# Seven and nine single rows in every step, from step -2 on, in a graph network's message passing

## The chip, the cores and the metric

The kernel runs on one core of a Trainium2 chip. The metric is the time of one execution on the device, in microseconds (us). Several executions are timed and the median is given; one more is recorded by the hardware profiler, and the profile is of that one. Engines are named as in the profile: PE is TensorE (matrix products), DVE is VectorE, ACT is ScalarE, POOL is GpSimd, SP is SyncE. SP, ACT and POOL also issue transfers (DMAs); a transfer's issue occupies the issuing engine's own instruction stream, the data move on their own.

## The reference

A graph has 12500 nodes with 64 features (`x`) and 200000 edges, sorted by target node (`dst`). Every edge computes a message from the features of its two ends and from its own 64 features, and the messages are summed at the target:

```python
nodes = node_state[edges].reshape(num_edges, -1)          # x[src], x[dst]: 128 values
gates = ssp(edge_state @ We1 + be1) @ We2 + be2
gates = gates * (1.0 - sigmoid(5.0 * (edges_distance - 3.5)))
h = ssp(nodes @ Wn1 + bn1) @ Wn2 + bn2
messages = h * gates
message_sum = zeros.at[edges[:, 1]].add(messages)
new_state = node_state + (ssp(message_sum @ Ws1 + bs1) @ Ws2 + bs2)
out = layernorm(x + new_state)
```

Here `ssp` is softplus less ln 2. What matters for the change is `x[src]`: the sources are random, so 200000 rows of 64 floats (256 bytes) have to be fetched one by one from memory. The targets are sorted, so neighbouring edges share a narrow window of nodes.

## The kernel before, in words

**Tiles and steps.** The edges are cut into 391 groups of 512 (`GE`); a group is one step `g`. A group has four tiles of 128 edges (`K = 4`), one edge to a partition. The last group has 192 edges of padding, and one of its tiles is padding alone.

**How the source rows come.** `gather(g)` lets POOL issue an indirect DMA for each of the four tiles (line 230): 128 row numbers from `src_i`, 128 rows of `x` into the tile `xg`. In the loop it is called 14 steps ahead (`AHEAD`); the gathers of steps 0 to 13 are issued in the preparation. For steps 5 to 17 the gather's tile is first touched by a small clearing on DVE (line 223, `after=True`), so that the gather takes its place behind what DVE did before. There are 18 buffers, and a later gather waits until the scatter of the step 18 back has read its buffer.

**Tiles by single rows.** Some tiles are not gathered by POOL. For these *slots* the rows are fetched one at a time by plain DMAs of 256 bytes from the queues of SP and ACT into a tile `xr` of their own (`fetch`, lines 232 to 255). Each row's byte address lies in a register; the registers are filled by an instruction that reads some values of `rows_i` from on-chip memory (the helper called at line 244 of the profile, `TENSOR_LOAD` there), and each DMA issue follows a short register move. Before the change a *piece* is four rows (`ROWS = 4`) with one reading of four values. SP fetches (3i + 4)//2 pieces up to step i, so one or two a step and six rows on the mean; ACT two pieces, eight rows, in each step. Both begin at step 0. `slots_by_rows` gives the slots: queue 0 (SP) takes tile 3 of a step, queue 1 (ACT) tile 2, always of the first step that lies at least 8 (SP) or 12 (ACT) steps (`READY`) behind the step in which the 128th row is issued. That makes 17 slots of SP and 23 of ACT, 40 in all, and 1523 gathers are left to POOL.

Each queue has two `xr` tiles, used in turn; the first row of a slot waits until the transposes of the slot two before have read the tile (`behind(ins, ("rows read", n - 2))`). The rows count up one of four semaphores for each queue (`landed`), and the transposes wait for the full count. `onehot` copies the tile's one-hot columns into `xr` on DVE (line 288).

**What a step computes.** `transposes(g)` (PE, line 299; line 296 for a slot's tile) turns rows and one-hot targets; `xcopy` (ACT, line 304) brings them to `xT`. `layer1_bias`, `layer1_edge` and `layer1_node` (PE, lines 309, 314, 320) make the first layer of both networks in `z`; the part of the target node comes from a window of 42 rows of a table made in the preparation, loaded for each half step as `wns` (SP, line 278; a register from `base_i`, line 273, says where). `exps` (ACT, 331), `logs` (ACT, 334) and `softplus` (DVE, 339) make the softplus; `layer2_edge` and `layer2_node` (PE, 345 to 354) the second layer; `hcut` and `message` (DVE, 363, 367) the message; `scatter` (PE, 371) and `window` (DVE, 388) add it to `sums`. When all edges of a block of 512 nodes are through, the parts of `node_block` are spread over the following steps.

**Order.** The order on each engine is the program's order, written out by hand (`tc.manual_schedule()`); an engine takes its instructions one after the other and stands still at one that has to wait. Loop step i, from -3 on, holds the first layer of step i+1, the transposes of step i+3, the second layer of step i and the scatter of step i-3. The first matmul of loop step i takes the waits for `xcopy(i+1)`, `load(i+1)` and gather and one-hot of step i+3. `load(i+5)` (SP) comes at the head of the loop step, `fetch` on SP follows it. On ACT the rows lie between the activations: two before `logs`, two after it, four after `xcopy`. The last ten steps (`CATCH_UP`) have another order and hold no fetches.

Of the kernel before, what the change touches and what calls it, by code (L numbers as in the profile page):

```python
# [44 lines left out]
I32 = mybir.dt.int32  # L45
U8 = mybir.dt.uint8
# [11 lines left out]
P = 128  # L58
D = 64
# [6 lines left out]
K = 4  # L66
# [7 lines left out]


BLOCK_STEPS = ((2, 3, 4, 4, 6, 7, 8, 9, 10, 14), (2, 3, 3, 4, 5, 6, 7, 8, 9, 10), (1, 2, 1, 2, 3))
ROWS = 4
READY = (8, 12)
LANDED = 4
CUTOFF = 5.0  # L80
# [20 lines left out]
    return steps  # L101


def pieces_by_row(i, queue):

    return max(0, 2 * i + 2 if queue else (3 * i + 4) // 2)
# [12 lines left out]


@with_exitstack
def gnn_resnorm_kernel(ctx: ExitStack, tc: tile.TileContext, a: dict, out: bass.AP, E: int):
    nc = tc.nc
    x = a["x"]
    N = x.shape[0]
# [73 lines left out]

    slots = slots_by_rows(NG)  # L200
    by_rows = {(g, k): n for n, (_, g, k) in enumerate(slots)}
    rows_i = const.tile([len(slots), P], I32, name="rows_i")
    queues = (nc.sync, nc.scalar)
    firsts = (0, len([1 for queue, _, _ in slots if queue == 0]), len(slots))
    landed = [[tc.alloc_semaphore(f"rows{queue}_{i}") for i in range(LANDED)] for queue in range(2)]
# [25 lines left out]
                out=xg[:, k, :D], out_offset=None, in_=x,  # L231
                in_offset=bass.IndirectOffsetOnAxis(ap=src_i[:, g, k : k + 1], axis=0)))

    def fetch(i, queue, piece, first=0, count=ROWS):

        if i < 0 or piece >= pieces_by_row(i, queue) - pieces_by_row(i - 1, queue):
            return
        n, r = divmod((pieces_by_row(i - 1, queue) + piece) * ROWS, P)
        n += firsts[queue]
        if n >= firsts[queue + 1]:  # L240
            return
        _, g, k = slots[n]
        if first == 0:
            _, row_at[queue] = nc.values_load_multi_w_load_instructions(  # L244
                rows_i[n : n + 1, r : r + ROWS], engines=[queues[queue].engine], min_val=0, max_val=4 * D * (N - 1),
                skip_runtime_bounds_check_because="src holds rows of x")
        if (n, "in") not in row_tiles:
            row_tiles[n, "in"], xrs[g, k] = row_tile(queue, n), row_tile(queue, n)
        for j in range(first, first + count):
            ins = queues[queue].dma_start(row_tiles[n, "in"][r + j : r + j + 1, :D].bitcast(U8),  # L250
                                          x_bytes[:, bass.ds(row_at[queue][j], 4 * D)])
            tc.no_tile_sem_insts.add(ins.ins.name)
            ins.then_inc(arrived(g, k)[0], 16)
            if r + j == 0:
                behind(ins, ("rows read", n - 2))

    row_at, row_tiles = {}, {}
# [220 lines left out]
    with tc.manual_schedule():  # L478
# [130 lines left out]
        with tc.tile_pool(name="finish", bufs=1) as finish:  # L609
# [24 lines left out]
            for i in range(-3, last - 1):  # L634
                now = parts.pop(i, [])
                early = [part for part in now if part.tensor]
                at(load, i + LOADS)
                fetch(i, 0, 0)
                fetch(i, 0, 1)
                if i >= 0:  # L640
                    at(gather, i + AHEAD, i < BEHIND)
                if i < ends:
                    needs = [("xcopy", i + 1), ("load", i + 1)]
                    needs += [(name, g) for g in ahead[i] for name in ("gather", "onehot")]
                    if i >= -1:
# [24 lines left out]
                    for g in third[i]:  # L670
                        window(g)
                    for part in early:
                        part.others()
                    at(softplus, i + 1)
                else:
                    for g in ahead[i]:
                        transposes(g)
                        xcopy(g)
                    layer1_bias(i + 1)
                    layer1_edge(i + 1)  # L680
                    for part in early:
# [149 lines left out]
def layouts(inputs):  # L831
# [18 lines left out]

    out = {"x": np.ascontiguousarray(x)}
    out["src_l"] = lanes(src, 0)
    out["rows"] = np.ascontiguousarray(out["src_l"].reshape(P, NG, K)[(slice(None), *list(zip(*slots_by_rows(NG)))[1:])].T)
# [45 lines left out]
```

## Time and profile before

| | us |
|---|---|
| median of 3 executions | 1969.16 |
| lowest, highest | 1963.82, 1975.15 |
| profiled execution | 1968.45 |
| its span in the profile | 1966.5 |
| POOL busy, 1523 gathers | 1444.8 |
| PE busy | 1750.5 |
| DVE, ACT busy | 1077.2, 922.5 |

The span is the time from the first to the last instruction that the profiler saw; the execution has 1.95 us around it. The busy time of an engine counts its computing instructions and POOL's gathers; issuing a DMA, register moves and readings of registers are not counted, so SP has no busy time at all, and ACT is occupied for longer than its row says. The page also lists 2176 row DMAs from SP and 2944 from ACT. In the views below, `PEld` is the loading of weights into PE, a `q` behind an engine's name means its instruction stream (ACTq: issued by ACT), and what stands in square brackets is the engine's idle time before the instruction and what ended it.

### The profile page before, as it was taken

How to read it: one execution, taken by the hardware profiler on the slowest of the kernel's cores; microseconds unless marked ns; L12 is line 12 of the kernel's file. 1: busy time of each engine (PE TensorE's matmuls, PEld its weight loads, DVE VectorE, ACT ScalarE, POOL GpSimd, SP SyncE). 2: the span in 40 equal slices, each digit the busy share in tenths (PEclk: the TensorE clock that was granted, in tenths of full speed). 3: DMA queues.
4: the chain of work that ended last, by engine and by line, in shares of the span. 5: the costliest groups of instructions: out<-in, count | busy, mean ns of one | idle time of the engine just before them, and what ended most of it. 6: DMA issues, size and time to landing. Idle time of an engine off the chain costs nothing.

```text
span 1966.5 us, 46634 instructions
## 1 busy us (share of the span) xinstructions
PE 1750.5 (89%) x11373; PEld 1491.4 (76%) x11373; DVE 1077.2 (55%) x2774; ACT 922.5 (47%) x1318; POOL 1445.0 (73%) x1527
## 2 busy tenths in 40 slices
PE   5899999999998988889889988998989989998896
PEld 4777877877777777777777777777777777777775
DVE  4455555555555555555555555555555555555654
ACT  1344545555454444445444444444544454444443
POOL 6777777777777777777777777777777777777770
PEclk9999999999999999999999999999999999999997
DMA  8422222222222222222222222222222222222220
GB/s 242 128 70 65 70 64 72 65 72 65 73 67 73 65 73 67 67 66 69 65 69 66 67 70 67 69 67 70 68 70 73 64 74 68 70 72 71 69 61 13
DMA packets 149240, 143.45 MB, mean 73 GB/s; under 512 B 50073, under 2 KB 96621, under 8 KB 148964
## 3 DMA queue, kind: packets, MB, share of 16 engines
q1 hardware_dynamic: 92972, 88.12, 15.6%
q0 software_dynamic: 48736, 50.00, 11.3%
q10 hardware_dynamic: 7256, 2.27, 0.6%
q8 instruction: 97, 1.59, 0.3%
q14 instruction: 179, 1.47, 0.3%
HBM read 130.59 MB, written 9.63 MB: 71 GB/s over the span
## 4 chain that ended last, share of the span: by engine, by line
PE 46%; ACTq 14%; DMA 10%; SPq 10%; issue 9%; ACT 5%; DVE 3%; POOL 3%; DVEq 0%; POOLq 0%
ACTq L250 11%; PE z L320 10%; PE gh L348 7%; PE gh L354 6%; PE z L314 5%; PE z L371 5%; DMA xg<-in_x,src_i 4%; PE tx L299 4%; DMA wns<-table 4%; SPq L250 4%; ACT u L331 3%; ACTq L244 3%; PE z L309 3%; POOL xg L230 3%; PE gh L345 2%
## 5 line engine op out<-in xcount | busy, mean ns | idle before, releaser
L230 POOL DMA_INDIRECT xg<-in_x,src_i x1523 | 1444.8, 949 | 475.3 <-issue 319.4
L331 ACT ACTIVATE u<-z 128x768 f32<-128x768 f32 x392 | 315.9, 806 | 624.4 <-PE z L371 316.7
L334 ACT ACTIVATE u<-u,one 128x768 f32<-128x768 f32 x392 | 366.0, 934 | 238.5 <-ACT u L331 236.7
L339 DVE SCALAR_TENSOR_TENSOR s<-u,z 128x768 f32<-128x768 f32 x392 | 372.6, 950 | 171.2 <-ACT u L334 154.6
L363 DVE TENSOR_TENSOR h<-gh,cut 128x256 f32<-128x256 f32 x391 | 165.2, 423 | 478.3 <-PE gh L354 472.0
L320 PE MATMUL z<-xT,wns 106*128 106x256 f32 x1564 | 423.9, 395 | 0.0
L354 PE MATMUL gh<-consts,s 128*128 128x64 f32 x3128 | 395.7, 270 | 0.0
L354 PEld LDWEIGHTS gh<-consts,s 128*128 128x128 f32 x3128 | 384.7, 194 | 0.0
L320 PEld LDWEIGHTS z<-xT,wns 106*128 106x128 f32 x1564 | 307.4, 198 | 45.8 <-ACT xT L304 0.7
L348 PEld LDWEIGHTS gh<-consts,s 128*128 128x128 f32 x1564 | 206.7, 192 | 122.8 <-issue 122.3
L348 PE MATMUL gh<-consts,s 128*128 128x128 f32 x1564 | 282.4, 304 | 0.0
L371 PEld LDWEIGHTS z<-xg,msg 128*128 128x128 f32 x1512 | 237.9, 199 | 22.9
L309 PE MATMUL z<-ones,be 3*128 3x256 bf16 x391 | 105.3, 269 | 167.8 <-DMA wns<-table 64.9
L299 PE MATMUL tx<-consts,xg 128*106 128x128 f32 x1524 | 240.8, 280 | 4.0 <-DVE xg L285 2.7
L388 DVE TENSOR_TENSOR sums<-sums,z 64x42 f32 x756 | 148.7, 197 | 171.4 <-ACT u L331 75.2
L314 PE MATMUL z<-eT,consts 128*128 128x256 f32 x782 | 242.4, 393 | 0.0
L304 ACT COPY xT<-tx 106x512 f32<-106x512 f32 x391 | 221.6, 567 | 15.5 <-PE tx L299 15.3
L371 PE MATMUL z<-xg,msg 128*128 128x84 f32 x1512 | 223.3, 271 | 0.0
L309 PEld LDWEIGHTS <-be 3*128 3x128 bf16 x391 | 35.4, 91 | 206.6 <-issue 102.9
L299 PEld LDWEIGHTS tx<-consts,xg 128*106 128x106 f32 x1524 | 181.8, 144 | 5.1 <-DVE xg L285 3.0
L367 DVE TENSOR_TENSOR msg<-gh,h 128x256 f32<-128x256 f32 x391 | 165.9, 424 | 13.4
L345 PE MATMUL gh<-row,ones 3*128 3x512 bf16 x391 | 145.9, 373 | 0.0
(103 smaller groups left out, 714.0 us busy)
## 6 DMA issues: line engine op xcount, KB each, us to landing
eT<-in_eT SPq DMA_DIRECT2D x195, 256.0 KB
xr<-in_x ACTq DMA_DIRECT2D x2944, 0.2 KB
xr<-in_x SPq DMA_DIRECT2D x2176, 0.2 KB
xg<-in_x,src_i POOLq DMA_INDIRECT x1523
wns<-table SPq DMA_DIRECT2D x782, 21.0 KB
table<-tb SPq DMA_DIRECT2D x14, 448.0 KB
sums<-in_xT SPq DMA_DIRECT2D x7, 455.0 KB
y<-in_x SPq DMA_DIRECT2D x24, 128.0 KB
```

Of the source, the lines that this page charges most:

```text
L230: note(("gather", g), nc.gpsimd.indirect_dma_start(out=xg[:, k, :D], out_offset=None, in_=x, in_offset=bass.IndirectOffsetOnAxis(ap=src_i[ ...
L250: ins = queues[queue].dma_start(row_tiles[n, "in"][r + j : r + j + 1, :D].bitcast(U8), x_bytes[:, bass.ds(row_at[queue][j], 4 * D)])
L299: nc.tensor.transpose(tx[:, k, :], xgs[g][:, k, :DW], ident)
L304: note(("xcopy", g), nc.scalar.copy(xT, xTs[g]))
L314: nc.tensor.matmul(zs[g][:, 0, :HE], we1.rearrange("a h d -> a (h d)"), eTs[g], start=False, stop=True, skip_group_check=True)
L320: nc.tensor.matmul(zn, wns[:, g % REST, h, :], xTs[g][:, h], start=True, stop=True, skip_group_check=True)
L331: nc.scalar.activation(us[g][:, part], z_of(g)[:, part], AF.Exp)
L334: nc.scalar.activation(us[g][:, part], us[g][:, part], AF.Ln, bias=one)
L339: nc.vector.scalar_tensor_tensor(ss[g].rearrange("p i t e -> p (i t e)")[:, part], us[g][:, part], BIG, z_of(g)[:, part], OP.min, OP.max)
L348: nc.tensor.matmul(v[:, 0, t], ss[g][:, 0, t, :], we2, start=False, stop=False, skip_group_check=True)
L354: nc.tensor.matmul(ghs[g][:, 1, 2 * t + h, :], ss[g][:, 1 + h, t, :], wn2, start=False, stop=h == 1 and t == 1, skip_group_check=True)
L371: ins = nc.tensor.matmul(sc, msgs[g][:, 2 * t : 2 * t + 2, :].rearrange("p h f -> p (h f)"), xgs[g][:, 2 * t : 2 * t + 2, D:DW], start=t = ...
```

## The change

A piece becomes 7 rows on SP and 9 on ACT (`ROWS`), one piece in every step from step -2 on (`ROWS_FROM`). One reading fills all the registers of a piece; it is a function of its own (`read_rows`), so that on ACT it stands between `exps` and `logs`, two rows behind `logs`, and seven behind `xcopy`. A piece may now run over the end of a slot into the next one. With `READY` as before there are 20 slots of SP and 26 of ACT, 46 in all, and 1517 gathers are left. There are 366 readings on SP and 370 on ACT, for 544 and 736 before. The row numbers lie in `rows_i` by pieces, one partition to a piece: 128 partitions of 48 columns, for 40 partitions of 128.

```diff
-ROWS = 4
+ROWS = (7, 9)
+ROWS_FROM = -2
 READY = (8, 12)
...
-            if pieces_by_row(g - READY[queue], queue) * ROWS >= (n + 1) * P:
+            if (g - READY[queue] - ROWS_FROM + 1) * ROWS[queue] >= (n + 1) * P:
...
+def row_pieces(NG):
+    queues = [queue for queue, _, _ in slots_by_rows(NG)]
+    return [-(-queues.count(queue) * P // ROWS[queue]) for queue in range(2)]
+
+def row_columns(NG):
+    return [-(-n // P) * rows for n, rows in zip(row_pieces(NG), ROWS)]
...
-    rows_i = const.tile([len(slots), P], I32, name="rows_i")
+    pieces_of, columns_of = row_pieces(NG), row_columns(NG)
+    rows_i = const.tile([P, sum(columns_of)], I32, name="rows_i")
...
-    def fetch(i, queue, piece, first=0, count=ROWS):
-        if i < 0 or piece >= pieces_by_row(i, queue) - pieces_by_row(i - 1, queue):
+    def read_rows(i, queue):
+        piece = i - ROWS_FROM
+        if not 0 <= piece < pieces_of[queue]:
             return
-        n, r = divmod((pieces_by_row(i - 1, queue) + piece) * ROWS, P)
-        ...
+        q, p = divmod(piece, P)
+        at = queue * columns_of[0] + q * ROWS[queue]
+        _, row_at[queue] = nc.values_load_multi_w_load_instructions(
+            rows_i[p : p + 1, at : at + ROWS[queue]], engines=[queues[queue].engine], min_val=0,
+            max_val=4 * D * (N - 1), skip_runtime_bounds_check_because="src holds rows of x")
+
+    def fetch(i, queue, first=0, end=None):
+        piece = i - ROWS_FROM
+        if not 0 <= piece < pieces_of[queue]:
+            return
-        for j in range(first, first + count):
+        for j in range(first, ROWS[queue] if end is None else end):
+            n, r = divmod(piece * ROWS[queue] + j, P)
+            n += firsts[queue]
+            if n >= firsts[queue + 1]:
+                return
...
                 at(load, i + LOADS)
-                fetch(i, 0, 0)
-                fetch(i, 0, 1)
+                read_rows(i, 0)
+                fetch(i, 0)
...
                     at(exps, i + 1)
-                    fetch(i, 1, 0, 0, ROWS // 2)
+                    read_rows(i, 1)
                     at(logs, i + 1)
-                    fetch(i, 1, 0, ROWS // 2, ROWS // 2)
+                    fetch(i, 1, 0, 2)
                     for g in ahead[i]:
                         transposes(g)
                         xcopy(g)
-                    fetch(i, 1, 1)
+                    fetch(i, 1, 2)
```

More of the change, by code (lines that the diff above doesn't have):

```diff
@@ L101, in block_steps @@
     return steps
-def pieces_by_row(i, queue):
-    return max(0, 2 * i + 2 if queue else (3 * i + 4) // 2)
 def slots_by_rows(NG):
@@ L232, in gather @@
                 in_offset=bass.IndirectOffsetOnAxis(ap=src_i[:, g, k : k + 1], axis=0)))
-    def fetch(i, queue, piece, first=0, count=ROWS):
-        if i < 0 or piece >= pieces_by_row(i, queue) - pieces_by_row(i - 1, queue):
+    def read_rows(i, queue):
+        piece = i - ROWS_FROM
+        if not 0 <= piece < pieces_of[queue]:
             return
-        n, r = divmod((pieces_by_row(i - 1, queue) + piece) * ROWS, P)
-        n += firsts[queue]
-        if n >= firsts[queue + 1]:
-            return
[L242 to L248, printed above, removed]
-        for j in range(first, first + count):
-            ins = queues[queue].dma_start(row_tiles[n, "in"][r + j : r + j + 1, :D].bitcast(U8),
+        q, p = divmod(piece, P)
[6 more added lines that the diff above has]
+        if not 0 <= piece < pieces_of[queue]:
+            return
+        for j in range(first, ROWS[queue] if end is None else end):
[3 more added lines that the diff above has]
+                return
+            _, g, k = slots[n]
+            if r == 0:
+                row_tiles[n, "in"], xrs[g, k] = row_tile(queue, n), row_tile(queue, n)
+            ins = queues[queue].dma_start(row_tiles[n, "in"][r : r + 1, :D].bitcast(U8),
                                           x_bytes[:, bass.ds(row_at[queue][j], 4 * D)])
@@ L253, in fetch @@
             ins.then_inc(arrived(g, k)[0], 16)
-            if r + j == 0:
+            if r == 0:
                 behind(ins, ("rows read", n - 2))
@@ L852, in layouts @@
     out["src_l"] = lanes(src, 0)
-    out["rows"] = np.ascontiguousarray(out["src_l"].reshape(P, NG, K)[(slice(None), *list(zip(*slots_by_rows(NG)))[1:])].T)
+    rows = []
+    for queue, (n, columns) in enumerate(zip(row_pieces(NG), row_columns(NG))):
+        chosen = [out["src_l"].reshape(P, NG, K)[:, g, k] for q, g, k in slots_by_rows(NG) if q == queue]
+        v = padded(np.concatenate(chosen), P * columns, 0).reshape(-1, P, ROWS[queue])
+        rows.append(v.transpose(1, 0, 2).reshape(P, columns))
+    out["rows"] = np.ascontiguousarray(np.concatenate(rows, axis=1))
     out["dst_l"] = lanes(dst, dst[-1])
```

## The prediction

> **What bounds the kernel now.** I read the busy shares and the costliest groups of the page first, then the gathers and the steps by stretch of time, then the order of single instructions where the stretches change.
>
> ```profile
> PE 1750.5 (89%) x11373; PEld 1491.4 (76%) x11373; DVE 1077.2 (55%) x2774; ACT 922.5 (47%) x1318; POOL 1445.0 (73%) x1527
> ...
> L230 POOL DMA_INDIRECT xg<-in_x,src_i x1523 | 1444.8, 949 | 475.3 <-issue 319.4
> ```
>
> By busy share TensorE (89%) looks like the bound and GpSimd (73%) does not. But GpSimd's idle time of 475.3 us over 1523 gathers is 0.31 us before each one, and most of it waits for nothing the profile knows ("issue"). So a gather costs 0.949 + 0.30 = 1.249 us, start to start. The same groups by stretch, columns: stretch, its length, busy time (instructions), granted clock, DMA share, GB/s; first the gathers, then the copies of `xT`, one for each step:
>
> ```profile
> core 0: us, POOL busy (x), PEclk, DMA share, GB/s
> 90.00:490.00 400.00, 302.56 (x320) 1.00 0.26 68
> 600.00:1000.00 400.00, 302.44 (x320) 0.97 0.26 68
> 1000.00:1400.00 400.00, 302.46 (x320) 0.96 0.27 68
> ```
>
> ```profile
> 90.00:490.00 400.00, 50.95 (x90) 1.00 0.26 68
> 600.00:1000.00 400.00, 46.99 (x83) 0.97 0.26 68
> 1000.00:1400.00 400.00, 46.34 (x82) 0.96 0.27 68
> ```
>
> GpSimd issues 320 gathers in each 400 us, early and late: 1.25 us each, never held up. The steps do change: 90 in 400 us early (4.44 us a step), then 82 or 83 (4.85). A step has 4 gathers less what the rows take over, 6/128 + 8/128 of one: 3.891 x 1.249 = 4.86 us. So until about 520 us the steps eat the lead of the gathers issued in the preparation (step 10 is copied 52 us after its last gather, step 100 nine); from there to about 1885 us GpSimd sets the pace. TensorE's first matmul of a step starts a median 1.9 to 2.3 us after the last gather it needs has left GpSimd, which is the landing (the last gathers are issued 1.3 us before their data arrive). The last gather leaves at 1920.6. The steps after about 1860 are paced by TensorE, ScalarE and VectorE in turn, hang on the gather of step 377, and give 46 us behind the last gather. GpSimd's one large halt is in the beginning:
>
> ```profile
> 79.19 0.94 POOL L230 DMA_INDIRECT xg<-in_x,src_i  x1 [0.30 <-issue]
> 84.75 0.94 POOL L230 DMA_INDIRECT xg<-in_x,src_i  x1 [4.61 <-DVE xg L223]
> ...
> 89.73 0.94 POOL L230 DMA_INDIRECT xg<-in_x,src_i  x1 [0.30 <-issue]
> ```
>
> The gather of step 14 (84.75) waits for VectorE's clearing of its tile, queued behind the first softplus, that behind ScalarE's first exponential. Whatever moves this moment moves the end by as much.
>
> **The change, part by part.** *Six gathers fewer* (46 slots for 40, all before step 380). On a queue that never pauses they are worth 6 x 1.249 = 7.5 us at the last gather. All six lie before the gather at which the last steps stop following GpSimd, so they start 7.5 us earlier too, with the same work: no row is fetched there before or after. Step pace: 3.875 x 1.249 = 4.84 us.
>
> *ScalarE.* Before, with two readings and eight rows:
>
> ```profile
> 1014.27 0.81 ACT L331 ACTIVATE u<-z 128x768 f32<-128x768 f32 x1 [1.52 <-PE z L371]
> 1015.09 0.77 ACTq L250 DMA_DIRECT2D xr<-in_x  x2
> 1015.90 0.94 ACT L334 ACTIVATE u<-u,one 128x768 f32<-128x768 f32 x1 [0.82 <-ACT u L331]
> 1015.98 0.54 ACTq L250 DMA_DIRECT2D xr<-in_x  x2
> 1016.75 0.56 ACT L304 COPY xT<-tx 106x512 f32<-106x512 f32 x1
> 1017.29 1.40 ACTq L250 DMA_DIRECT2D xr<-in_x  x4
> 1018.78 0.81 ACT L331 ACTIVATE u<-z 128x768 f32<-128x768 f32 x1 [1.48 <-DVE s L339]
> ```
>
> 1.63 us from exponential to logarithm, 0.85 to the copy, 2.03 to the next exponential: 4.51. After: only the reading stands before the logarithm, and if it is shorter than the exponential (0.81) the logarithm follows after 0.84, as at the first step, where nothing stood between; two rows lie beside the logarithm (0.84 to the copy); seven rows of 0.313 (1.40 for four, of which 0.23 is the first one's extra behind a reading) take 2.2, with 0.1 around them. Sum 3.98 us: shorter than before, hidden under 4.84. Were that cover gone, the extra row would cost 0.31 a step, less the saved reading. Behind the seven rows queues the next exponential, for which VectorE's softplus and TensorE's second layer wait; that is latency inside a step with 0.8 us to spare.
>
> *SyncE.* A piece of four is reading 0.61 with its gap, 0.07, rows 1.24, 0.05: 1.97 us, 1.5 pieces a step: 2.96. Besides it each step issues half an `eT` load and half a reading of `base_i` (0.45 + 0.54 for two steps), two window loads (0.92), and now and then a `y` or `out` (0.05): 4.41 in all. After: one reading (0.65, next part, and 0.05), 0.07, seven rows (1.24 x 7/4 = 2.17), 0.05: 2.99, in all 4.44. Against 4.84 there is 0.40 to spare. SyncE's window loads are issued a median 29 us before TensorE needs them in the middle, about 10 us early on: either covers the two extra pieces (6 us), and an early delay only shortens the lead that the steps have to use up.
>
> *One reading of seven or nine values* is not in the trace. Columns: least, median, most ns:
>
> ```profile
> L244 ACTq TENSOR_LOAD <-rows_i x736: 478/558/762, 84.0 to 1831.0; - x184
> L244 SPq TENSOR_LOAD <-rows_i x544: 463/564/776, 83.6 to 1791.8; - x182
> ```
>
> ```profile
> L754 ACTq TENSOR_LOAD <-far_i x1: 467/467/467, 1959.9 to 1959.9; - x1
> ```
>
> Four values take 558 or 564 ns, one takes 467 (477 on SyncE): some 30 ns a value more. I take that slope: nine 0.71 us, seven 0.65. Low end: no growth (`base_i`, also four values, has 0.49). High end, time in proportion to values: 1.26 and 0.99. At the high end ScalarE has 3.98 + 1.26 - 0.81 = 4.43 and SyncE 4.78: both still under 4.84, SyncE barely.
>
> The Trainium skill, page "Runtime: NRT & Kernel Launch", section "Instruction fetch mechanics", speaks against this change: register loading costs about 200 ns a register, in its example from HBM. By that rule, as an estimate, a seven-value reading is 1.4 us, SyncE's step 5.19 us, and SyncE would set the pace from 80 us on: 366 pieces end near 1980, and with the 141 us that followed the same step before, the time would be some 2120 us. For four values the rule gives 0.80 us where the row has 0.56, and the numbers here go by the row.
>
> *Two steps earlier.* Each queue gets two more pieces ahead of step 0, where ScalarE stood idle: its copies at 75.27 and 76.12, then nothing until 81.44 (4.74 us, waiting for TensorE). The first nine rows (0.71 + 9 x 0.313 + 0.23 = 3.8 us) fit before 81.44. The second nine push the next exponential from 84.00 to about 85.4 and its logarithm by 0.75, so VectorE's clearing for step 15 goes from 87.67 to about 88.4; GpSimd wants it at 89.73. Bounds: zero, and 7.5 us if both pieces stood whole in GpSimd's way; a gain is excluded, as nothing that the clearing waits for gets shorter. I take zero, by these rows. On SyncE the extra pieces stand behind the loads of steps 0 to 3; the loads of steps 4 and 5 go 3 and 6 us later, to about 87 and 89, for steps near 95 and 99.
>
> *Rows in time, and the rest.* SyncE's pieces of a tile are issued 8 steps before its step, ScalarE's 12; the transposes come 3 before. A tile's first row waits for the tile two slots earlier, whose transposes lie at least five steps back. Six more copies of 0.19 us on VectorE (55% busy), six transposes that read another tile: nothing. Scaling the row numbers over 128x48 for 40x128: nothing.
>
> **Sum.** Span 1966.5 - 7.5 = 1959.0. The profiled execution lasted 1968.45, 1.95 more than its span and 0.7 under the median 1969.16, so its successor is 1961.0, and on the median 1961.7 us (-0.38%).
>
> **Rivals.** *SyncE becomes the bound* (slower). Point: a seven-value reading over 1.05 us (0.65 + 0.40), or as much lost in rows; each 0.1 us beyond costs 366 x 0.1 = 37 us. At 1.2 us: 55 more, about 2017. For it: SyncE's 4.41 of 4.86 is the next fullest queue. Against it: the 30 ns slope. Chance 0.10.
>
> *The beginning eats the gain.* If the earlier pieces stand in GpSimd's way, up to 7.5 us return: 1965 to 1969. For it: a chain of three engines behind 84.75 and only 1.3 us of margin at step 15. Against it: the 4.74 us idle. Chance 0.09.
>
> *The last steps are also quicker.* Behind 1885 TensorE had a mean clock of 0.85 for 81 us, 12 us of full clock withheld; at the middle's 0.97 it would be 2.4. A third of the difference is 3.3 us: 1953 to 1959. Against it: nothing in the change asks for it, and it can as well go the other way. Chance 0.28, the spread of the median included.
>
> **How the numbers follow.** The forecast has 0.53. The range: lowest run less 7.5 and 3.3 is 1953; highest run less 7.5 plus 3.3 is 1971. It leaves out SyncE's case and some edges. A difference within 0.5% (9.8 us) is about what cannot be told from none: faster by more takes the quicker end, 0.28; within, forecast and beginning, 0.62; slower, SyncE, 0.10.
>
> **What would show it.** 1517 gathers at 1.25 us with the last one leaving near 1913 and no new pause; the wait near 79 us as long as before; readings of 0.65 to 0.71 us; the logarithm 0.84 us behind the exponential; 46 us behind the last gather. The prediction is wrong if gathers pause in the middle, if SyncE's window loads come due late, or if step 14's gather starts later than 85.

## The result and the profile after

The changed kernel takes **2286.77 us** (median of 4 executions, 2285.56 to 2295.49), beside 1972.16 us for the kernel before, measured with it (4 executions, 1963.82 to 1979.13): a ratio of 1.161, with a 95% interval of 1.1585 to 1.1644. (The ratios here are the recorded ones; they can differ by up to 0.002 from the quotient of the two medians.) The forecast was 1961.7 us, its range 1953 to 1971. The profiled execution of the changed kernel has a span of 2285.0 us, 318.5 more than before.

The page of the changed kernel, its busy times, the gathers' group and the chain that ended last:

```profile
PE 1935.6 (85%) x11373; PEld 1628.4 (71%) x11373; DVE 1069.1 (47%) x2780; ACT 947.2 (41%) x1318; POOL 1439.9 (63%) x1521
...
ACTq 46%; PE 24%; issue 14%; ACT 12%; DVE 2%; DMA 1%; SPq 0%; DVEq 0%
ACTq L266 29%; ACTq L249 17%; ACT u L347 8%; PE z L336 5%; PE gh L370 4%; PE gh L364 3%; PE z L330 2%; PE z L387 2%; ACT xT L320 2%; PE tx L315 2%; PE z L597 1%; PE gh L361 1%; PE z L325 1%; PE tx L423 1%; ACT u L350 1%
...
L238 POOL DMA_INDIRECT xg<-in_x,src_i x1517 | 1439.7, 949 | 752.4 <-issue 378.6
```

No engine's computing explains 318 us: TensorE's same 11373 matmuls took 185 us more at a lower granted clock, ScalarE's work 25 more. GpSimd issues its 1517 gathers at 949 ns as before but stands idle for 752 us in place of 475. The chain now runs through ScalarE's instruction stream (ACTq), 46% of the span: the row issues of line 266 and, at 17%, the reading of the row numbers, line 249. The gathers of the changed kernel by stretch (stretch, length, busy time and count, granted clock, DMA share, GB/s), then the copies of `xT`, one for each step:

```profile
90.00:490.00 400.00, 268.12 (x285) 0.88 0.25 59
600.00:1000.00 400.00, 260.25 (x276) 0.88 0.24 57
1000.00:1400.00 400.00, 261.33 (x277) 0.90 0.24 58
```

```profile
90.00:490.00 400.00, 42.14 (x72) 0.88 0.25 59
600.00:1000.00 400.00, 41.57 (x71) 0.88 0.24 57
1000.00:1400.00 400.00, 42.15 (x72) 0.90 0.24 58
```

Where 320 gathers left in every 400 us, 276 to 285 leave now, and a step takes 400/72 = 5.6 us from the very beginning. GpSimd no longer sets the pace; it has its lead and waits for buffers that the scatters free, 293 us in all behind line 387's matmuls (the columns of the view of waits: us in total, times, longest):

```profile
POOL xg L238 <- PE z L387: 293.3, 170, 5.5
```

Steps 10 to 128 took 4.53 us each before and 5.59 now, steps 128 to 250 4.88 and 5.63, steps 250 to 370 4.87 and 5.67: 124 + 92 + 97 = 313 us of the 318.5.

What lengthened the step is seen in the readings (least, median, most ns) and in the order of ScalarE's instructions:

```profile
L249 ACTq TENSOR_LOAD <-rows_i x370: 2132/2220/2442, 72.5 to 2150.1; - x185
L249 SPq TENSOR_LOAD <-rows_i x366: 1092/1739/1897, 77.4 to 2127.9; - x183
```

```profile
1007.91 0.81 ACT L347 ACTIVATE u<-z 128x768 f32<-128x768 f32 x1 [1.75 <-DVE h L379]
1010.20 0.94 ACT L350 ACTIVATE u<-u,one 128x768 f32<-128x768 f32 x1 [1.48 <-issue]
1010.56 0.78 ACTq L266 DMA_DIRECT2D xr<-in_x  x2
1011.37 0.58 ACT L320 COPY xT<-tx 106x512 f32<-106x512 f32 x1 [0.24 <-PE gh L370]
1011.45 2.10 ACTq L266 DMA_DIRECT2D xr<-in_x  x7
1013.65 0.81 ACT L347 ACTIVATE u<-z 128x768 f32<-128x768 f32 x1 [1.69 <-DVE h L379]
```

A reading of nine values takes 2.22 us, not 0.71, and one of seven 1.09 to 1.90, not 0.65. The logarithm (line 350) follows the exponential by 2.29 us, 1.48 of them ScalarE's own idle time, in which it stands at the reading. Then come 1.17 us to the copy and 2.28 to the next exponential: 5.74 us.

### The profile page after: what moved, and what is told of

Its sections match the earlier page's. It is cut to its first block, busy times and chain, and to the rows that moved or that the text cites. A ratio compares the mean times of both kernels' runs of the same rounds, so it can differ in the third digit from the quotient of the medians.

```text
span 2285.0 us, 47623 instructions
## 1 busy us (share of the span) xinstructions
PE 1935.6 (85%) x11373; PEld 1628.4 (71%) x11373; DVE 1069.1 (47%) x2780; ACT 947.2 (41%) x1318; POOL 1439.9 (63%) x1521
## 4 chain that ended last, share of the span: by engine, by line
ACTq 46%; PE 24%; issue 14%; ACT 12%; DVE 2%; DMA 1%; SPq 0%; DVEq 0%
ACTq L266 29%; ACTq L249 17%; ACT u L347 8%; PE z L336 5%; PE gh L370 4%; PE gh L364 3%; PE z L330 2%; PE z L387 2%; ACT xT L320 2%; PE tx L315 2%; PE z L597 1%; PE gh L361 1%; PE z L325 1%; PE tx L423 1%; ACT u L350 1%
## 5 line engine op out<-in xcount | busy, mean ns | idle before, releaser
L336 PE MATMUL z<-xT,wns 106*128 106x256 f32 x1564 | 496.6, 449 | 0.0
L336 PEld LDWEIGHTS z<-xT,wns 106*128 106x128 f32 x1564 | 357.0, 230 | 66.2 <-ACT xT L320 0.7
L370 PE MATMUL gh<-consts,s 128*128 128x64 f32 x3128 | 403.1, 273 | 0.0
L370 PEld LDWEIGHTS gh<-consts,s 128*128 128x128 f32 x3128 | 393.9, 198 | 0.0
L364 PEld LDWEIGHTS gh<-consts,s 128*128 128x128 f32 x1564 | 224.9, 207 | 129.6 <-issue 128.9
L364 PE MATMUL gh<-consts,s 128*128 128x128 f32 x1564 | 306.9, 323 | 0.0
L387 PEld LDWEIGHTS z<-xg,msg 128*128 128x128 f32 x1512 | 267.8, 221 | 32.2
L330 PE MATMUL z<-eT,consts 128*128 128x256 f32 x782 | 275.9, 440 | 0.0
L315 PE MATMUL tx<-consts,xg 128*106 128x128 f32 x1518 | 253.5, 291 | 14.6 <-ACT xT L320 10.2
L387 PE MATMUL z<-xg,msg 128*128 128x84 f32 x1512 | 245.4, 290 | 0.0
L315 PEld LDWEIGHTS tx<-consts,xg 128*106 128x106 f32 x1518 | 193.9, 153 | 18.8 <-ACT xT L320 12.9
```

The costliest lines, as they stand in the source:

```text
L315: nc.tensor.transpose(tx[:, k, :], xgs[g][:, k, :DW], ident)
L330: nc.tensor.matmul(zs[g][:, 0, :HE], we1.rearrange("a h d -> a (h d)"), eTs[g], start=False, stop=True, skip_group_check=True)
L336: nc.tensor.matmul(zn, wns[:, g % REST, h, :], xTs[g][:, h], start=True, stop=True, skip_group_check=True)
L364: nc.tensor.matmul(v[:, 0, t], ss[g][:, 0, t, :], we2, start=False, stop=False, skip_group_check=True)
L370: nc.tensor.matmul(ghs[g][:, 1, 2 * t + h, :], ss[g][:, 1 + h, t, :], wn2, start=False, stop=h == 1 and t == 1, skip_group_check=True)
L387: ins = nc.tensor.matmul(sc, msgs[g][:, 2 * t : 2 * t + 2, :].rearrange("p h f -> p (h f)"), xgs[g][:, 2 * t : 2 * t + 2, D:DW], start=t = ...
```

## The experiments

The question is why a reading of seven or nine values costs that much, and whether that is all.

**1. Readings by themselves.** To the kernel before, behind its steps, readings of 1 to 12 values are added, four of each, from a place in `rows_i` that starts at a 16-byte bound, and from one or two values (4 or 8 bytes) further on. Each value read is used by one row DMA. Its time as a whole says nothing. The changed kernel's own readings differ in their start: SyncE's pieces begin 0, 7 or 14 values into a partition of 48, ScalarE's 21, 30 or 39.

```diff
+            v = rows_i[0:1, 16:48]
+            for _ in range(4): use(read(v[:, 0:1], engines=[SP])[1], 0)
...
+            for _ in range(4): use(read(v[:, 0:7], engines=[SP])[1], 0)
+            for _ in range(4): use(read(v[:, 0:8], engines=[SP])[1], 0)
...
+            for _ in range(4): use(read(v[:, 1:8], engines=[SP])[1], 0)
+            for _ in range(4): use(read(v[:, 2:10], engines=[SP])[1], 0)
...
+            for _ in range(4): use(read(v[:, 1:10], engines=[ACT])[1], 1)
```

> The kernel before, with readings of 1 to 12 values appended on SyncE ahead of the last stores, four of each kind, each at its own line, and six kinds on ScalarE; each reading is followed by as many row transfers into a spare tile. Words are counted from a 64-byte bound; 'at +1' begins one 4-byte word behind it. In the changed kernel's own trace SyncE's seven values take 1.2 us where the piece begins at word 0 of the tile and 1.75 us where it begins at word 7 or 14; ScalarE's nine (words 21, 30, 39) take 2.2 us. Theory A, alignment: from a 16-byte bound four values come together for the price of about one, every other value costs 0.22 us by itself, and from any other start all values come singly. By it: 1 value 0.47 us, 4 values 0.56, 5 values 0.78, 6 values 1.0, 7 values 1.2, 8 values 0.65 to 0.8, 9 values 0.9 to 1.0, 12 values 0.75 to 1.0; 4 values at +1 or +2 1.0, 7 at +1 or +2 1.75, 8 at +2 2.0, 9 at +1 2.2. Theory B, number: whatever the start, up to four values cost 0.56 and beyond four each value costs 0.22 to 0.25: 8 values 1.4 to 2.0 and 12 values 2.3 to 2.9 from a 16-byte bound too, and 4 at +1 stays 0.56. Theory C, crossing a 32-byte line is what costs: 7 at +1 (words 1 to 7, no line crossed) would take 1.2 us, 9 from the bound 2.2.

The readings of that kernel on SyncE, least, median and most ns; in order 1, 2, 4, 7, 8, 9 and 12 values from a bound, then 4 and 7 values starting one further on and 8 starting two further on:

```profile
L733 SPq TENSOR_LOAD <-rows_i x4: 475/492/497, 1939.6 to 1942.8; - x4
L734 SPq TENSOR_LOAD <-rows_i x4: 725/728/868, 1943.7 to 1948.2; - x4
...
L736 SPq TENSOR_LOAD <-rows_i x4: 557/562/566, 1957.8 to 1963.6; - x4
...
L739 SPq TENSOR_LOAD <-rows_i x4: 1180/1186/1186, 1988.1 to 1998.7; - x4
L740 SPq TENSOR_LOAD <-rows_i x4: 783/784/943, 2002.3 to 2013.2; - x4
L741 SPq TENSOR_LOAD <-rows_i x4: 996/1004/1017, 2016.7 to 2028.7; - x4
L742 SPq TENSOR_LOAD <-rows_i x4: 1007/1023/1053, 2033.1 to 2048.1; - x4
L743 SPq TENSOR_LOAD <-rows_i x4: 1117/1131/1166, 2053.1 to 2061.0; - x4
...
L745 SPq TENSOR_LOAD <-rows_i x4: 1721/1725/1727, 2073.6 to 2085.9; - x4
...
L747 SPq TENSOR_LOAD <-rows_i x4: 1927/1927/1928, 2106.6 to 2120.4; - x4
```

Eight values take less than seven, and twelve hardly more than nine. Four and one are nearly alike, two are 0.24 us more than one. So the time goes not by values but by what is called an access here: some 0.27 us, and on SyncE 0.20 to 0.29 for each group of four that starts at a bound or each single value, estimates from these rows. The traces show times alone; that a group comes in one piece is read out of them. Seven from a bound are one group and three singles: 0.27 + 4 x 0.23 = 1.19 us, measured 1.186. Started off a bound, the time is that of every value read singly: seven 0.27 + 7 x 0.21 = 1.74, measured 1.725. ScalarE's readings follow the same law, up to 6% longer (nine from a bound 1.064 us, nine started one further on 2.244). Theory A stands, those by the number alone (B) or by a 32-byte line (C) fall. The changed kernel's readings of 1.2 us (SyncE's first 128), 1.75 (the rest) and 2.22 (ScalarE) are the same three cases.

**2. The readings from a bound, then padded, then cut to four.** In the first kernel each piece starts at a bound, and seven and nine values are read as in the changed kernel. In the second, eight and twelve values are read there, whole groups. In the third, four are read, and the rows beyond the fourth use these four addresses again: it leaves out the reading of the other three or five.

```diff
+WIDTH = (8, 12)
...
-    return [-(-n // P) * rows for n, rows in zip(row_pieces(NG), ROWS)]
+    return [-(-n // P) * width for n, width in zip(row_pieces(NG), WIDTH)]
...
-        at = queue * columns_of[0] + q * ROWS[queue]
+        at = queue * columns_of[0] + q * WIDTH[queue]
...
```

The second has this and

```diff
-            rows_i[p : p + 1, at : at + ROWS[queue]], engines=[queues[queue].engine], min_val=0,
+            rows_i[p : p + 1, at : at + WIDTH[queue]], engines=[queues[queue].engine], min_val=0,
```

The third has the first's edit and

```diff
-            rows_i[p : p + 1, at : at + ROWS[queue]], engines=[queues[queue].engine], min_val=0,
+            rows_i[p : p + 1, at : at + 4], engines=[queues[queue].engine], min_val=0,
...
-                                          x_bytes[:, bass.ds(row_at[queue][j], 4 * D)])
+                                          x_bytes[:, bass.ds(row_at[queue][j % 4], 4 * D)])
```

> The changed kernel, each piece's row numbers beginning at a multiple of 16 bytes (pieces 8 and 12 words apart instead of 7 and 9); the readings still take seven and nine values. Theory A: SyncE reads in 1.2 us, ScalarE in 0.9 to 1.0. ScalarE's step becomes about 4.3 us, SyncE's 1.45 + 1.2 + 2.4 = 5.05 us, which is over GpSimd's 4.84: SyncE sets the pace and the time is 2035 to 2060 us. Theory B: readings as in the changed kernel, 1.75 and 2.2 us, ScalarE at 5.6 us a step, 2280 us.

> As the kernel with aligned pieces, but each reading takes the whole padded piece, eight values on SyncE and twelve on ScalarE, of which seven and nine are used. Theory A: 0.65 to 0.8 us and 0.75 to 1.0 us; ScalarE about 4.2 us a step, SyncE about 4.5, both under GpSimd's 4.84; the six gathers saved show, and the time is 1958 to 1966 us, 0.3 to 0.4% under the kernel before. Theory B: more values, so slower than the changed kernel: readings of 2.0 and 2.9 us, ScalarE at 6.3 us a step, about 2540 us.

> The changed kernel with one reading of four values from a 16-byte bound for each piece; the fifth to ninth rows of a piece are fetched from the addresses of the first to fifth again, so the output is not the reference's. It leaves the readings at 0.56 us and everything else of the change as it is: seven and nine rows, two steps earlier, 46 slots. If the length of the readings is the whole cause, the time is 1961 us, plus or minus 6 (ScalarE about 4.0 us a step, SyncE 4.4). If the order on ScalarE, the extra rows or the earlier start cost something of their own, it stays above 1985 us.

| kernel | SyncE's reading, us | ScalarE's reading, us | time, us | ratio to the kernel before (1976.81), 95% interval |
|---|---|---|---|---|
| seven and nine from a bound | 1.21 | 0.97 | 2111.43 | 1.0693 (1.0675 to 1.0711) |
| eight and twelve from a bound | 0.81 | 0.99 | 1971.02 | 0.9981 (0.9961 to 1.0) |
| four from a bound | 0.57 | 0.49 | 1964.78 | 0.9941 (0.9924 to 0.9958) |

The readings are medians of these rows, of the first, second and third kernel:

```profile
L250 ACTq TENSOR_LOAD <-rows_i x370: 947/973/1224, 75.2 to 1974.0; - x185
L250 SPq TENSOR_LOAD <-rows_i x366: 1099/1213/1402, 80.1 to 1967.8; - x183
```

```profile
L250 ACTq TENSOR_LOAD <-rows_i x370: 950/985/1184, 74.6 to 1836.0; - x185
L250 SPq TENSOR_LOAD <-rows_i x366: 703/807/961, 79.5 to 1830.1; - x183
```

```profile
L250 ACTq TENSOR_LOAD <-rows_i x370: 478/491/742, 74.5 to 1827.5; - x185
L250 SPq TENSOR_LOAD <-rows_i x366: 467/571/754, 79.5 to 1794.0; - x183
```

Reading one value *more* on SyncE, which makes two whole groups (and three more on ScalarE, where it changes the reading by 0.01 us), takes 140 us off the time. In the first kernel SyncE alone is the bound, as its chain says:

```profile
SPq 50%; PE 25%; issue 12%; DMA 5%; ACTq 2%; DVE 2%; ACT 2%; POOL 1%; DVEq 0%; POOLq 0%
```

Its time lies above the 2035 to 2060 expected. The steps take 5.10 us (10 to 128) and 5.19 (128 to 370), where SyncE's sum is 4.44 - 0.65 + 1.21 = 5.00: the sum misses 0.1 to 0.2 us a step. In the padded kernel the same holds: sum 4.60, steps 4.70 (10 to 128) and 4.79 (128 to 250), a chain with 38% on SyncE's stream, and from step 40 to 360 a step's first window load is issued between 2.7 us after that step's copy of `xT` and 4.3 us before it. Its time, 1971.02 us, lies above the 1958 to 1966 expected too, and it is 0.2% under the kernel before where 0.3 to 0.4% was expected. Most of what the sum misses stands in SyncE's own rows. Between 200 and 600 us of the first kernel, seven rows with their register moves take 2.38 us a step as a mean, where the sum had 2.29, and a semaphore instruction, 0.07 with its gap, stands in none of its terms. With four addresses the lead of the window loads grows to 27 us at step 200 (25 in the kernel before), and GpSimd is the pace again; the time lies inside the 1961 plus or minus 6 expected. Its start, the gathers around the halt:

```profile
78.45 0.95 POOL L239 DMA_INDIRECT xg<-in_x,src_i  x1 [0.31 <-issue]
84.06 0.95 POOL L239 DMA_INDIRECT xg<-in_x,src_i  x1 [4.66 <-DVE xg L232]
...
89.06 0.95 POOL L239 DMA_INDIRECT xg<-in_x,src_i  x1 [0.30 <-issue]
```

Halted for 5.61 us (5.56 before), it starts again 0.7 us earlier than before; the step after has no second halt. So the 46 slots, the seven and nine rows in every step and the two earlier pieces cost nothing that shows once the reading is short: the whole loss is the reading.

**3. One queue at a time.** In the first kernel here ScalarE's pieces are padded to twelve values and start at a bound, SyncE's lie as in the changed kernel. In the second SyncE's are padded to eight, ScalarE's nine start off a bound. Both have the changed kernel's rows and steps. The first's edit is shown; the second has `WIDTH = (8, 9)` and `GAP = 1`.

```diff
+WIDTH = (7, 12)
+GAP = 3
...
-        at = queue * columns_of[0] + q * ROWS[queue]
+        at = queue * (columns_of[0] + GAP) + q * WIDTH[queue]
...
-            rows_i[p : p + 1, at : at + ROWS[queue]], engines=[queues[queue].engine], min_val=0,
+            rows_i[p : p + 1, at : at + WIDTH[queue]], engines=[queues[queue].engine], min_val=0,
...
```

They were run three times. Twice the chip was another, on which the kernel before itself took 2459 and 2503 us, so that these runs are no measure of the question; the third time it took 1973.77 us. The expectations of the first two:

> Only SyncE keeps the expensive readings: ScalarE's nine row numbers start at a 16-byte bound and are read as twelve values (0.99 us in the padded kernel, against 2.22 in the changed one); SyncE's seven lie as in the changed kernel (1.2 us where they start at a bound, 1.75 elsewhere). Theory A (each of the two queues was by itself slow enough): SyncE's step is 4.44 us with 0.65 for the reading, so 5.54 with 1.75; with the 0.13 by which the aligned kernel's step came out above its sum, 5.67. In the first 128 of some 370 steps the reading is 1.2 us as in the aligned kernel, 5.13 to 5.2 a step. So 1965 + 128 x 0.33 + 240 x 0.83 = some 2205 us (2170 to 2240), SyncE's window loads with hardly any lead, the readings of ScalarE under 1.1 us. Theory B (ScalarE alone was the bound of the changed kernel, SyncE only followed it): within 1% of the padded kernel's 1971 us.

> Only ScalarE keeps the expensive readings: SyncE's seven row numbers start at a 16-byte bound and are read as eight values (0.81 us in the padded kernel, against 1.75); ScalarE's nine lie off the bounds as in the changed kernel (2.22 us). Theory A (each queue was by itself slow enough): ScalarE's step is 3.98 us with 0.71 for the reading, so 5.49 with 2.22; the changed kernel's own rows give 5.5 to 5.7 (2.3 from exponential to logarithm, 0.9 to 1.2 to the copy, 2.3 to the next exponential). Over 370 steps that is 1965 + 370 x 0.65 to 0.86 = 2205 to 2285 us, with SyncE's window loads far ahead (30 us or more). Theory B (SyncE alone was the bound, ScalarE only followed it): within 1% of the padded kernel's 1971 us.

> The same kernel as e_act (only SyncE keeps the expensive readings: seven numbers as in the changed kernel, 1.2 us where they start at a 16-byte bound and 1.75 elsewhere; ScalarE reads twelve from a bound in 0.97), now beside a kernel before that takes some 1970 us. Theory A (SyncE alone was slow enough): 4.44 us less 0.65 plus 1.75 is 5.54 a step, with 0.13 for stalls as in the aligned kernel 5.67; 5.13 to 5.2 in the first 128 steps. 1965 + 128 x 0.33 + 240 x 0.83 = some 2205 us (2170 to 2240, a ratio of 1.10 to 1.135). Theory B (ScalarE alone was the bound, SyncE only followed it): within 1% of the padded kernel's 1971 us.

> The same kernel as e_sp (only ScalarE keeps the expensive readings: nine numbers off the bounds, 2.2 us; SyncE reads eight from a bound in 0.8), now beside a kernel before that takes some 1970 us. Theory A (ScalarE alone was slow enough): 3.98 us less 0.71 plus 2.22 is 5.49 a step, by the changed kernel's rows 5.5 to 5.7: 2205 to 2285 us, a ratio of 1.12 to 1.16, SyncE's window loads 30 us or more ahead. Theory B (SyncE alone was the bound): within 1% of 1971 us. Theory C (ScalarE's step has cover that the sum leaves out, since its exponential waits for TensorE and not for the reading in some steps): 4.9 to 5.4 us a step, 1990 to 2170 us.

On these two chips the ratios were 1.118 and 1.1165 with SyncE's long readings, in steps of 6.5 to 7.0 us. With ScalarE's they were 1.036 and 1.034, far under the 1.12 to 1.16 expected; but there the steps took 6.1 to 6.5 us, more than the 5.6 of ScalarE's stream, so that most of its reading could lie hidden. In their traces SyncE's register moves ahead of the row issues, 29 ns as a mean in the padded kernel, average 0.10 to 0.13 us, single ones up to 1.5 us, while ScalarE's exponential (0.81 us) and GpSimd's gathers (1.25 us start to start where nothing holds them) are as long as elsewhere. The granted clock of the kernel before was 0.85 to 0.87 there, 0.96 to 0.97 on the others. Why is not known, and the kernel before has no trace there; that a kernel that asks less of SyncE loses less there is all that they show.

> The kernel of e_act and act_12 (only SyncE keeps the expensive readings; ScalarE reads twelve values from a 16-byte bound in 0.97 us). Those two ran where the kernel before itself took 2459 and 2503 us. Beside a kernel before of some 1970 us, theory A (SyncE's readings alone were enough): 5.1 to 5.2 us a step in the first 128 steps and 5.5 to 5.7 after, 2170 to 2240 us, a ratio of 1.10 to 1.135. Theory B (ScalarE alone was the bound): within 1% of 1971 us.

> The kernel of e_sp and sp_8 (only ScalarE keeps the expensive readings, 2.2 us; SyncE reads eight values from a 16-byte bound in 0.8), beside a kernel before of some 1970 us. Theory A (ScalarE's readings alone were enough): 5.5 to 5.7 us a step, 2205 to 2285 us, a ratio of 1.12 to 1.16, SyncE's window loads 30 us or more ahead. Theory B (SyncE alone was the bound): within 1% of 1971 us. Theory C (part of ScalarE's reading is covered by waits that it had before): 4.9 to 5.4 us a step, 1990 to 2170 us.

With SyncE's long readings alone the time is 2231.33 us, a ratio of 1.130 (1.1263 to 1.133). Its readings, its chain, and its copies of `xT` by stretch:

```profile
L251 ACTq TENSOR_LOAD <-rows_i x370: 949/978/1280, 75.3 to 2095.1; - x185
L251 SPq TENSOR_LOAD <-rows_i x366: 1101/1738/1968, 80.2 to 2088.7; - x183
```

```profile
SPq 42%; PE 30%; issue 11%; DMA 7%; POOL 4%; DVE 2%; ACT 2%; ACTq 1%; DVEq 0%; POOLq 0%
```

```profile
200.00:600.00 400.00, 45.64 (x78) 0.94 0.26 62
800.00:1200.00 400.00, 41.20 (x71) 0.89 0.24 58
1200.00:1600.00 400.00, 40.96 (x70) 0.91 0.24 58
```

78 steps in 400 us (5.13 us each) while the readings still start at a bound, then 70 or 71 (5.6 to 5.7) when they do not: the law of experiment 1 seen as a change of pace within one run. With ScalarE's long readings alone the time is 2283.38 us, a ratio of 1.157 (1.1532 to 1.1611), all but that of the changed kernel:

```profile
L251 ACTq TENSOR_LOAD <-rows_i x370: 2134/2217/2548, 75.1 to 2150.4; - x185
L251 SPq TENSOR_LOAD <-rows_i x366: 705/806/969, 81.1 to 2109.8; - x183
```

```profile
ACTq 47%; PE 24%; issue 14%; ACT 12%; DVE 1%; DMA 1%; SPq 0%; DVEq 0%
```

```profile
200.00:600.00 400.00, 42.14 (x72) 0.88 0.24 57
800.00:1200.00 400.00, 41.72 (x72) 0.90 0.24 58
1200.00:1600.00 400.00, 41.55 (x71) 0.91 0.25 59
```

72 steps in 400 us from the start, as in the changed kernel, and SyncE's window loads 30 to 36 us ahead of the copies from step 60 on. So each queue's readings were by themselves enough to take the pace, and theory A holds for both, inside the expected times. ScalarE's cost 52 us more, and the difference lies in the first 128 steps (5.59 us a step for 5.09), in which SyncE's readings still start at a bound; ScalarE's 370 all start off one. SyncE's cost was hidden beside them, all but: in the changed kernel the lead of its window loads falls from 33 us at step 100 to 16 at step 350.

**4. Kernels meant to beat both.** SyncE's rows are counted in whole groups, eight a piece, with no piece in one step of six (the first) or of four (the second); ScalarE has nine (the first) or ten rows (the second) and reads twelve values. Shown is the first's edit; its lines for the wider readings are those of the padded kernel. The second has `ROWS = (8, 10)` and `EVERY = 4`.

```diff
-ROWS = (7, 9)
+ROWS = (8, 9)
+WIDTH = (8, 12)
+EVERY = 6
...
+def pieces_to(i, queue):
+    n = max(0, i - ROWS_FROM + 1)
+    return n if queue else n - n // EVERY
...
-        piece = i - ROWS_FROM
-        if not 0 <= piece < pieces_of[queue]:
+        piece = pieces_to(i, queue) - 1
+        if not pieces_to(i - 1, queue) <= piece < pieces_of[queue]:
...
```

> A kernel meant to be quicker than both: SyncE fetches eight rows, read as eight values from a 16-byte bound (0.78 us by the appended readings), in five of six steps and nothing in the sixth; ScalarE nine in every step, read as twelve values from a bound (0.99). 46 slots, 1517 gathers as in the changed kernel. SyncE's work of a step falls against the padded kernel by a sixth of a reading and a third of a row (0.13 + 0.10 us), so that its window loads should gain a lead of 20 us or more, as in the kernel with four addresses. Theory: 0.4 to 0.6% under the kernel before (ratio 0.994 to 0.996), last gather within 3 us of 1915. Rival: the padded kernel's ratio of 0.998 comes from ScalarE's longer reading (0.99 against 0.49 with four addresses), not from SyncE; then 0.998 again.

> One slot more than in the kernel with eight rows in five of six steps: SyncE eight rows in three of four steps, ScalarE ten in every step (twelve values read, from a 16-byte bound): 47 slots, 1516 gathers. One gather fewer is 1.25 us (0.06%). ScalarE's tenth row costs it 0.31 us a step, in steps of 4.85 us where its work is some 4.6. Theory: ratio 0.993 to 0.996, not told apart from the kernel with 46 slots or 1 us quicker. Rival: ScalarE's step becomes as long as the gathers' (the copy of each step later by 0.3), and the time is 5 to 40 us above that of 46 slots.

> The same kernel as v1 (SyncE eight rows in five of six steps, read as eight values from a 16-byte bound; ScalarE nine in every step, read as twelve; 46 slots), now beside a kernel before that takes some 1970 us. SyncE's work of a step falls against the padded kernel by 0.23 us. Theory: SyncE's barely kept pace was what held the padded kernel at a ratio of 0.998; here 0.994 to 0.996. Rival: ScalarE's longer reading (0.97 against 0.49 with four addresses) was; then 0.998 again.

> The same kernel as v2 (SyncE eight rows in three of four steps, ScalarE ten in every step, read as twelve values; 47 slots, 1516 gathers), now beside a kernel before that takes some 1970 us. Theory: a ratio of 0.993 to 0.996, not told apart from 46 slots. Rival: ScalarE's step, 0.31 us longer, becomes as long as the gathers' 4.85, and the time is 5 to 40 us above that of 46 slots.

> The kernel of v2 and v2_four (SyncE eight rows in three of four steps, ScalarE ten in every step; 47 slots, 1516 gathers), beside a kernel before of some 1970 us. Theory: a ratio of 0.993 to 0.996, as with four addresses a reading. Rival: ScalarE's step, by its tenth row and its longer reading some 4.6 us, becomes as long as the gathers' 4.85, and the ratio is 0.998 or more.

On the two other chips the first had ratios of 1.017 and 1.012, where 0.994 to 0.996 or 0.998 were expected, the second 1.000 and 0.993 (0.9907 to 0.9954). Beside a kernel before of 1973.77 us only the second was run: **1964.83 us, a ratio of 0.9957 (0.9938 to 0.9976)**, as expected, 47 slots, SyncE's window loads 23 to 30 us ahead of the copies from step 60 on. Its readings:

```profile
L257 ACTq TENSOR_LOAD <-rows_i x372: 950/995/1250, 75.4 to 1837.8; - x186
L257 SPq TENSOR_LOAD <-rows_i x288: 712/805/977, 81.2 to 1879.7; - x144
```

ScalarE's tenth row did not make it the pace: GpSimd issues 319 or 320 gathers in 400 us throughout. The kernel is quicker than the changed one by 14%, and than the one before by a little (0.2 to 0.6%). Whether the first would be so beside a kernel before of 1974 us is open.

## Why the prediction was wrong, point by point

**One reading of seven or nine values: the step that failed.** "Some 30 ns a value more" was a slope between one value and four. All four-value readings of the kernel before began at a bound, so one and four are one access each, and the slope compares an access with an access. Measured: 2.22 us for nine and 1.2, then 1.75, for seven, where 0.71 and 0.65 stood. The high end, "in proportion to values", 1.26 and 0.99, was no bound either: it scales up four values that came at the price of one access, and so lies below every reading that is made singly, and it left the start of the reading out. The trace of the kernel before held the row that says so, on VectorE. Two readings of it, of two values and of one:

```profile
L379 DVEq TENSOR_LOAD <-base_i x391: 522/528/797, 97.2 to 1945.5; - x196
```

```profile
L754 DVEq TENSOR_LOAD <-far_i x1: 311/311/311, 1960.8 to 1960.8; - x1
```

0.217 us for the second value. A slope from these two, from one value to seven and nine, would have given 0.47 + 6 x 0.217 = 1.8 us on SyncE and 0.47 + 8 x 0.217 = 2.2 on ScalarE, which are the measured sizes of the readings off a bound.

**The rule that was weighed and set aside.** The Trainium skill, page "Runtime: NRT & Kernel Launch", section "Instruction fetch mechanics", has about 200 ns for loading a register. This case agrees for values that are read singly (0.20 to 0.24 us each, on the fixed 0.27), and not for whole groups (eight values 0.78 us, not 1.6). Its estimate in the prediction, some 2120 us, came out low: it had 1.4 us for SyncE where 1.75 was measured, and put nothing on ScalarE. By the same rule, as an estimate, nine values are 1.8 us there, and ScalarE's step some 5.0 against the gathers' 4.84.

**ScalarE.** The condition was right ("if it is shorter than the exponential (0.81) the logarithm follows after 0.84"): with the reading of 0.49 the logarithm follows after 0.83 to 0.85, with one of 0.99 after 1.08, in the changed kernel after 2.29. Seven rows and the next exponential were priced at 2.3 and take 2.28. So ScalarE's 3.98 less 0.84 and plus 2.29 is 5.43, beside 5.6 measured. (The 5.49 of the expectations takes 0.71 off, which is no term of 3.98: a reading that short lies beside the exponential.) That this queue could become the bound was no rival in the prediction, since its high end was 4.43, and the change's step pace of 4.84 us fell with it. Of the three signs of being wrong that the prediction named, only the pauses of the gathers in the middle appeared; the other two watch SyncE and the beginning, and none watches ScalarE's stream.

**SyncE becomes the bound.** The rival named the right mechanism, but its point, 1.05 us, was too high. The budget of 4.44 us (its terms add up to 4.46) misses 0.1 us a step up to step 128 and 0.13 to 0.2 later, mostly the rows and the semaphore instruction named in experiment 2, and so the 0.40 to spare were 0.2 to 0.3: a reading of 0.81 already has SyncE barely keeping up. Its price, 37 us for each 0.1, holds beyond that: from 0.81 to 1.21 us 140 us, or 35 for each 0.1. In the changed kernel itself SyncE was not the bound: its window loads stayed 15 us or more ahead from step 20 on, and its share of the chain is 0%. ScalarE came first, and SyncE's readings alone would have been enough.

**Six gathers fewer.** Right, as far as the runs can tell: with four addresses 1517 gathers that nothing held up behind the halt, the last leaving at 1917.6, and 45.4 us behind it (46 foretold). The forecast of 1913 for the last gather was 4.5 us early; in that run a gather took 1.255 us start to start as a mean for 1.252 before, which over some 1460 gathers is that much. The time, 0.59% under the kernel before (0.42 to 0.76), is if anything better than the 0.38 forecast.

**Two steps earlier, rows in time, and the rest.** Priced at nothing, and nothing they cost with short readings (experiment 2). In the changed kernel itself the halt was longer, by the same readings:

```profile
76.43 0.94 POOL L238 DMA_INDIRECT xg<-in_x,src_i  x1 [0.30 <-issue]
83.51 0.94 POOL L238 DMA_INDIRECT xg<-in_x,src_i  x1 [6.14 <-DVE xg L231]
...
89.06 0.94 POOL L238 DMA_INDIRECT xg<-in_x,src_i  x1 [0.87 <-DVE xg L231]
```

7.08 us from issue to issue for 5.56 before, and 0.87 us of waiting at the gather of step 15. The beginning that "eats the gain" did not: GpSimd started again 1.2 us earlier than before, and in these steps it is no longer what counts. The last steps were no quicker where they can be compared: with four addresses 45.4 us lie behind the last gather, for 46 before. (A third of 12 less 2.4 is 3.2 us, not the 3.3 of that rival.)

## What to carry to other kernels

In these runs an instruction that reads several registers from on-chip memory costs by its accesses (seven values off a bound 1.73 us, eight from one 0.78). So lay the values out so that each reading starts at a 16-byte bound and takes whole groups of four, even where some values are read for nothing. When two rows of a trace give a slope, ask first what they have in common beside the quantity that is varied; a third row, here two values on VectorE, would have shown that one against four was no slope. A queue that issues transfers between computing instructions needs a budget of its own: its readings and issues count in no busy share, and here they took the bound from an engine at 73%.

## What the runs showed of the hardware that was not expected

- A reading's time on SyncE: some 0.27 us and 0.20 to 0.29 for each access; seven values 1.19 us from a bound and 1.73 off it, eight 0.78 and 1.93.
- TensorE's granted clock fell from 0.96 to 1.00 in the kernel before to 0.88 to 0.90 in the changed one, with the same matmuls: they were busy 1936 us in place of 1750. Where SyncE's or ScalarE's stream set the pace, it was 0.88 to 0.94 as well. Longer pauses between the matmuls and the lower clock come together here; which makes which was not tried.
- On two chips the unchanged kernel took 2459 and 2503 us where others took 1972 to 1977, at a granted clock of 0.85 to 0.87 in place of 0.96 to 0.97; SyncE's register moves took 0.10 to 0.13 us there for 0.03.
